# One exponential for the softmax weights of two key tiles in an attention loop

## The chip, the core and the metric

The kernel runs on one core of one Trainium2 chip. The metric is the device time of one execution in microseconds (us), lower is better. The engines are named as in the profile: PE (TensorE, the matrix engine), PEld (its weight loads), DVE (VectorE), ACT (ScalarE), POOL (GpSimd) and SP (SyncE, which here only issues DMAs).

## The reference

Four images of 64 x 64 positions with 256 channels go through two layers. The first is a deformable convolution with a residual. The second takes each image as 4096 tokens and adds an attention and then a gated feed-forward block. The change lies in the attention alone:

```python
def _L1_attn_ref(inputs, Wt, Wx, bh, Wa, ba):
    q = jnp.einsum('bld,du->blu', inputs, Wt)
    k = jnp.einsum('bld,ud->blu', inputs, Wx)
    beta = jnp.tanh(q[:, :, None, :] + k[:, None, :, :] + bh)
    alpha = jnp.einsum('bqku,u->bqk', beta, Wa[:, 0]) + ba[0]
    a = jax.nn.softmax(alpha, axis=-1)
    c_r = jnp.einsum('bqk,bkd->bqd', a, inputs)
    return c_r
...
t = t + _L1_attn_ref(_ln_t(t), L1_attn_Wt, L1_attn_Wx, L1_attn_bh, L1_attn_Wa, L1_attn_ba)
```

For each pair of a query and a key the score is a weighted sum of 32 hyperbolic tangents; the softmax over keys then weights the tokens.

## The kernel before

The images are handled one after the other. For each there is a stage of preparation and then the attention loop, `attention(n, v, [sampling])`. While the loop of image n runs, pieces of the sampling of image n + 1 (the convolution of the first layer) are mixed in as "side" work; the last image has no successor, so its loop runs without side work.

The scores are not made with tanh. The 32 units are split into six groups, taken as three "pairs"; in each group the sum of the tanh terms is a quotient of two sums that PE can make as matrix products. For one key tile (128 keys) and one block of 512 queries, the kernel does for each pair p = 1, 2, 3:

- D: PE makes the denominators d (128 x 1024, two PSUM banks; `below_line`), and N: the numerators nn (two halves of 128 x 512, named a and b; `above_line`). Pairs 1 and 2 take two matmuls for d and one for each half of nn, pair 3 twice that.
- L and E: ACT turns d into 1/d as exp(-ln d): a logarithm (line 1289) writes a new buffer r from d, an exponential (line 1291) works on r in place.
- m: DVE multiplies each half of r with its nn (`quotient`, line 1207).

Then the three r are added: s12 (POOL, line 1295) adds the second to the first, s3a (POOL, line 1297) and s3b (DVE, line 1299) add the third in two halves, and sum (DVE, line 1302) adds the two halves of 512 columns into a buffer et. W (`weigh`) is the exponential of et in place, on ACT (line 1214): these are the softmax weights of the key tile. V (`gather_values`) lets PE multiply weights with values (line 1230): groups of eight key tiles are collected, and for each of four rows of queries the eight tiles are summed in PSUM, two tiles in each V and two V in each step. `hand_over` ("out", once a step) adds a finished sum to acv on DVE (line 1252, or 1250 for the first group of a query block), or, where nothing is finished, takes up one waiting item of the end of a query block: a divide (lines 1261 and 1262, which needs a tile tr loaded by SP), or row statistics.

There are 8 query blocks with 32 key tiles each, so 256 steps ("tiles" b) in the loop of one image and 1024 in the program. The order on each engine is written out as lanes of operations with lags in tiles, and a small planner pops them in turn; nearly every instruction is held in that order. ACT's lane is the first one:

```python
        order = [
            [("L2", 0), ("L1", 0), ("E2", 0), ("E1", 0), ("L3", 0), ("E3", 0), ("W", 2)],
            [("N1a", 1), ("D2", 0), ("N1b", 1), ("Va", 3), ("N2a", 1), ("D1", 0), ("N2b", 1), ("N3a", 1), ("Vb", 3),
             ("D3", 0), ("N3b", 1), ("fill", 0)],
            [("m1a", 1), ("m1b", 1), ("m2a", 1), ("side", 0), ("s3b", 2), ("again", 1), ("m2b", 1), ("sum", 2),
             ("m3a", 1), ("m3b", 1), ("out", 3)],
            [("s12", 1), ("s3a", 1)],
        ]
```

So on ACT the weight exponential of tile b stands between the third exponential of tile b + 2 and the first logarithm of tile b + 3. On DVE the side work of the sampling (copies at lines 828 and 909, products and sums of gathered rows at lines 779 and 783) stands between the product m2a and s3b.

The buffers that matter: d has two (of two banks each), nn two banks, r six (`rp`, three for each tile), et 17 of 2 KB per partition (`ep`, 2 x 8 + 1), tr four of 1 KB. Loads of keys (kf), queries (qf) and tr are issued by SP in its own order.

Of the kernel before, what the change touches and what calls it, by code (L numbers as in the profile page):

```python
# [10 lines left out]
F32 = mybir.dt.float32  # L11
R32 = mybir.dt.float32r
I32 = mybir.dt.int32
AF = mybir.ActivationFunctionType
# [4 lines left out]
P = 128  # L19
NB, H, W, C = 4, 64, 64, 256  # L20
# [21 lines left out]
PVB = 8  # L42
# [9 lines left out]
def layers_kernel(ctx: ExitStack, tc: tile.TileContext, a, out: bass.AP):  # L52
    nc = tc.nc
# [109 lines left out]
    with tc.tile_pool(name="selp", bufs=1) as sp, tc.tile_pool(name="ps_c", bufs=2, space=PSUM) as ps_c:  # L163
# [16 lines left out]
        acc = sp.tile([P, P], F32, name="acc")  # L180
# [59 lines left out]
    def rows(i):  # L240
        return slice(i * P, (i + 1) * P)
# [4 lines left out]
    S = SimpleNamespace(gather=True, hold=False, fills=None, left=0, tables=[], listing=True)  # L246

    @contextmanager
    def scope(*pools):

        with ExitStack() as st:
            for name, bufs, psum in pools:
                kw = {"space": PSUM} if psum else {}
                setattr(S, name, st.enter_context(tc.tile_pool(name=name, bufs=bufs, **kw)))
            yield
            for name, _, _ in pools:
                delattr(S, name)

    keep = tc.keep_in_program_order
# [722 lines left out]
    def row_stats(mv, row, vec=nc.vector):  # L982
        st = S.sb.tile([P, 6], F32, tag="st", name="st2")
        vec.bn_stats(st, row)
        vec.bn_aggr(mv, st)
# [143 lines left out]
    def attention(n, v, beside):  # L1129
# [58 lines left out]
        def below_line(b, pair):  # L1188

            d = S.ps_d.tile([P, 2, 512], F32, tag="d", name="d")  # L1190
            for j in range(2):
                product(d[:, j, :], b, 0, 2 * pair - 2 + j)
            if pair == 3 and b % NT == NT - 1 and b + 1 < nb:
                for which, p in ((0, 3), (1, 1), (1, 2)):
                    queries(b // NT + 1, which, p)
            return d

        def above_line(b, pair, j):

            nn = S.ps_n.tile([P, 512], F32, tag="n", name="nn")  # L1200
            product(nn, b, 1, 2 * pair - 2 + j)
            if pair == 3 and j == 1 and b % NT == NT - 1 and b + 1 < nb:
                queries(b // NT + 1, 1, 3)
            return nn

        def quotient(r, nn, j):
            keep(nc.vector.tensor_tensor(r[:, j, :], nn, r[:, j, :], ALU.mult))  # L1207

        ets, acc, pend, due, rest, late = {}, {}, [], [], [], [0]

        def weigh(b):
            keep(nc.scalar.activation(ets[b], ets[b], AF.Exp))  # L1214
            size = tail.get(b, PVB if b % PVB == PVB - 1 and b < nb - PVB else 0)
            if size:
                pend.extend((b - size + 1, size, j, h) for j in range(4) for h in range(size // 2))
# [18 lines left out]
        def hand_over():  # L1236

            if not due:
                if rest:
                    if len(rest) == late[0]:  # L1240
                        late[0] -= 1
                    rest.pop(0)()
                return
            q, k0, last, j, pv = due.pop(0)
            if j == 0 and k0 == 0:
                ac_t = S.ap.tile([P, 4, C + 1], F32, tag="acv", name="acv")
                acc["sum"] = ac_t
            ac = acc["sum"]
            if k0 == 0:
                keep(nc.vector.tensor_copy(ac[:, j, :], pv))  # L1250
            else:
                keep(nc.vector.tensor_add(ac[:, j, :], ac[:, j, :], pv))  # L1252
            if last:
                i = 4 * q + j
                tr = S.sb.tile([P, C], F32, tag="tr", name="tr", bufs=4)
                nc.sync.dma_start(out=tr, in_=t_d[n][rows(i)])
                t2 = S.sb.tile([P, C], F32, tag="tt", name="t2", bufs=4)

                def divide():
                    es = S.sb.tile([P, 1], F32, tag="es", name="es")  # L1260
                    keep(nc.vector.reciprocal(es, ac[:, j, C:]))
                    keep(nc.vector.scalar_tensor_tensor(t2, ac[:, j, :C], es, tr, ALU.mult, ALU.add))
                    nc.sync.dma_start(out=t2_d[n][rows(i)], in_=t2)

                rest.insert(len(rest) - late[0], divide)
                rest.append(lambda: row_stats(tmv[:, i, :], t2, pinned))
                late[0] += 1
# [9 lines left out]
        rs, ds, ns = {}, {}, {}  # L1277

        def emit(op, b):

            nonlocal second
            p = int(op[1]) if op[1:2].isdigit() else 0
            if op[0] == "D":
                ds[b, p] = below_line(b, p)
            elif op[0] == "N":
                ns[b, op] = above_line(b, p, "ab".index(op[2]))
            elif op[0] == "L":
                rs[b, p] = S.rp.tile([P, 2, 512], F32, tag="r", name="r")
                keep(nc.scalar.activation(rs[b, p], ds.pop((b, p)), AF.Ln))  # L1289
            elif op[0] == "E":  # L1290
                keep(nc.scalar.activation(rs[b, p], rs[b, p], AF.Exp, scale=-1.0))  # L1291
            elif op[0] == "m":
                quotient(rs[b, p], ns.pop((b, "N" + op[1:])), "ab".index(op[2]))
            elif op == "s12":
                keep(nc.gpsimd.tensor_tensor(rs[b, 1], rs[b, 1], rs[b, 2], ALU.add))  # L1295
            elif op == "s3a":
                keep(nc.gpsimd.tensor_tensor(rs[b, 1][:, 0], rs[b, 1][:, 0], rs[b, 3][:, 0], ALU.add))  # L1297
            elif op == "s3b":
                keep(nc.vector.tensor_add(rs[b, 1][:, 1], rs[b, 1][:, 1], rs[b, 3][:, 1]))  # L1299
            elif op == "sum":  # L1300
                et = S.ep.tile([P, 512], F32, tag="et", name="et")
                keep(nc.vector.tensor_add(et, rs[b, 1][:, 0], rs[b, 1][:, 1]))  # L1302
                ets[b] = et
            elif op == "W":
                weigh(b)
            elif op[0] == "V":
                gather_values()
            elif op == "out":
                hand_over()
            elif op == "side":  # L1310
                emit("fill", b)
                for side in beside:
                    next(side, None)
            elif op == "fill":
                while S.fills:
                    S.fills.pop(0)()
            elif op == "again":
                second += max(S.left / max(nb - 6 - b, 1) - 1, 0)
                if second >= 1:
                    second = min(second - 1, 1)  # L1320
                    emit("side", b)
# [38 lines left out]
        for step in range(nb + 4):  # L1360
# [6 lines left out]
            while True:  # L1367
                went = False
                for lane in lanes:
                    while lane and ready(*lane[0]):  # L1370
                        op, b = lane.pop(0)
# [353 lines left out]
    for n in range(NB):  # L1725
        with scope(("att", 1, 0), ("smp", 2, 0), ("dn", 1, 0)):
            v = S.att.tile([P, NT, C + 1], F32, name="v")

            sampling = sample_image(n + 1) if n + 1 < NB else iter(())
            S.gather, S.hold = False, True  # L1730
            with scope(
                ("one", 1, 0), ("two", 2, 0), ("sb", 2, 0), ("row", 2, 0), ("rp", 11, 0),
                ("ps_d", 2, 1), ("ps_n", 1, 1), ("ps_m", 3, 1),
            ):


                main = feed_forward(n - 1, pinned) if n else iter(())
                prep = attention_prep(n, v, pinned)
                listing = (list_tokens(i) for i in range(1, NB))
                if n:  # L1740
                    turns = (
                        "mos" + "m" * 3 + "mo" * 8 + "om" + "oss" * 2 + "m" + "o" * 10 + "m" + "o" * 3
                        + ("m" + "o" * 3 + "m" * 4) * 3
                    )
                else:
                    turns = "oo" + "ool" * 3 + "oo" + "s" + "os" * 24
                for turn in turns:
                    next({"m": main, "o": prep, "s": sampling, "l": listing}[turn], None)
                for rest in (main, prep):
                    for _ in rest:  # L1750
                        pass
            S.gather, S.hold = True, False
            with scope(
                ("two", 2, 0), ("sb", 2, 0), ("ep", 2 * PVB + 1, 0), ("rp", 6, 0), ("ap", 1, 0), ("qp", 16, 0), ("kp", 4, 0),
                ("ps_d", 2, 1), ("ps_n", 2, 1), ("ps_v", 1, 1), ("ps_m", 1, 1),
            ):
                attention(n, v, [sampling])
        attention_any(n)
        if n + 1 < NB:
            sample_any(n + 1)  # L1760
# [39 lines left out]
```

## Time and profile before

| what | value |
|---|---|
| median of 3 runs | 9245.01 us (9230.27 to 9249.85) |
| the profiled execution | 9240.03 us, span 9238.3 us |
| busy share of the span | PE 88%, DVE 77%, ACT 79%, POOL 55% |
| weight exponential, line 1214 | 1024 instructions, mean 614 ns, 628.7 us busy |
| exponential of r, line 1291 | 3072 instructions, mean 1055 ns, 3133.3 us busy |
| logarithm, line 1289 | 3072 instructions, mean 1015 ns, 3066.3 us busy |
| attention loops, first to last weight exponential | 1317 to 2996, 3343 to 5021, 5371 to 7047, 7388 to 8974 us |

The four loops take together some 6.6 of the 9.2 ms. Shares over the whole span are averages over unlike stages, so the loops are read by themselves. A row's duration runs from the start of an instruction to its last write; where two follow each other on ACT, the second starts before the first has ended, so the distance from start to start is what an instruction costs its engine. In the timelines a row "x2" is two instructions of one kind in a stretch, with the time of the whole; what stands in square brackets is idle time ahead of the row and what ended it.

### The profile page before, as it was taken

The page shows a single profiled execution, that of the slowest core. Times are in us where ns is not written, and L with a number is a line of the kernel's source. Part 1 is how long each engine was busy: PE and PEld are TensorE (multiplying, and loading weights), DVE is VectorE, ACT ScalarE, POOL GpSimd, SP SyncE. Part 2 cuts the span into 40 slices and gives each one's busy share as a digit, 9 for nine tenths or more (in the row PEclk, how much of TensorE's full clock was granted, in tenths as well). Part 3 has the DMA queues.
Part 4 walks back from the last instruction along what each step waited for, and adds up shares of the span by engine and source line. Part 5 has one row for each costly group of instructions (what it writes and reads, how often), then busy time and mean ns, then how long its engine had stood idle before and what let it go on. Part 6 is the DMA issues. An engine that isn't in the chain of part 4 may idle for free. (4 is left out here: it accounts for less than half of the span.)

```text
span 9238.3 us, 139629 instructions
## 1 busy us (share of the span) xinstructions
PE 8127.6 (88%) x46154; PEld 5830.1 (63%) x46154; DVE 7094.9 (77%) x13053; ACT 7294.4 (79%) x8590; POOL 5075.3 (55%) x3108
## 2 busy tenths in 40 slices
PE   5777779999999599999997799999996899999995
PEld 3555547777776267777775367777774466666663
DVE  4545559998988569999987479999987388888872
ACT  2344269999999379999997489999996499999982
POOL 0122247777766157777764267777663266666652
PEclk8888779999999799999999799999998899999997
DMA  3455565555542545555533555555533533333322
GB/s 113 133 165 166 156 203 153 152 149 151 153 131 87 201 148 153 152 149 157 157 117 98 188 151 154 159 153 154 145 110 105 193 102 105 103 103 103 112 71 83
DMA packets 1575709, 1279.14 MB, mean 138 GB/s; under 512 B 123522, under 2 KB 1407140, under 8 KB 1574948
## 3 DMA queue, kind: packets, MB, share of 16 engines
q1 hardware_dynamic: 1411940, 958.70, 35.0%
q10 hardware_dynamic: 123264, 190.67, 5.7%
q0 software_dynamic: 39744, 120.42, 5.6%
q8 instruction: 379, 6.21, 0.3%
q14 instruction: 382, 3.13, 0.1%
HBM read 1011.33 MB, written 285.79 MB: 140 GB/s over the span
## 5 line engine op out<-in xcount | busy, mean ns | idle before, releaser
L1207 DVE TENSOR_TENSOR r<-nn,r 128x512 f32<-128x512 f32 x6144 | 4107.5, 686 | 716.9 <-PE nn L1184 522.8
L1295 POOL TENSOR_TENSOR r<-r 128x1024 f32<-128x1024 f32 x1024 | 2719.7, 2656 | 1727.5 <-DVE r L1207 1350.6
L1184 PE MATMUL nn<-qf,kf 128*128 128x512 f32 x8192 | 3221.9, 441 | 201.0 <-DVE r L1207 67.5
L1289 ACT ACTIVATE r<-d 128x1024 f32<-128x1024 f32 x3072 | 3066.3, 1015 | 277.9 <-DVE r L1299 177.1
L1291 ACT ACTIVATE r<-r 128x1024 f32<-128x1024 f32 x3072 | 3133.3, 1055 | 32.5
L1184 PE MATMUL d<-qf,kf 128*128 128x512 f32 x8192 | 2546.7, 412 | 48.7 <-ACT r L1289 31.9
L1184 PEld LDWEIGHTS nn<-qf,kf 128*128 128x128 f32 x8192 | 1454.3, 188 | 1197.2 <-DVE r L1207 889.1
L1230 PE MATMUL pv<-v,et 128*128 128x257 f32 x8192 | 2143.2, 384 | 35.5 <-DVE acv L1252 35.5
L1230 PEld LDWEIGHTS pv<-v,et 128*128 128x128 f32 x8192 | 1527.9, 190 | 353.1 <-DVE acv L1252 52.7
L1184 PEld LDWEIGHTS d<-qf,kf 128*128 128x128 f32 x8192 | 1491.4, 189 | 392.3 <-ACT r L1289 117.5
L1297 POOL TENSOR_TENSOR r<-r 128x512 f32<-128x512 f32 x1024 | 1333.1, 1302 | 83.9 <-DVE r L1207 3.9
L1299 DVE TENSOR_TENSOR r<-r 128x512 f32<-128x512 f32 x1024 | 715.6, 699 | 14.0 <-POOL r L1295 13.8
L1302 DVE TENSOR_TENSOR et<-r 128x512 f32<-128x512 f32 x1024 | 703.4, 687 | 10.3 <-POOL r L1297 10.3
L767 POOL DMA_INDIRECT ga<-xt,tii x576 | 588.2, 1021 | 207.3 <-issue 84.3
L1214 ACT ACTIVATE et<-et 128x512 f32<-128x512 f32 x1024 | 628.7, 614 | 22.3 <-DVE et L1302 22.3
L871 PE MATMUL ptq<-ident,wq 128*120 128x128 f32 x2048 | 313.4, 281 | 80.9 <-ACT ac L830 48.0
L871 PEld LDWEIGHTS ptq<-ident,wq 128*120 128x120 f32 x2048 | 291.0, 183 | 133.7 <-ACT ac L830 49.8
L913 POOL TENSOR_TENSOR xr<-ac,xr 128x256 f32<-128x256 f32 x32 | 27.5, 859 | 558.6 <-ACT ac L912 558.5
L270 PE MATMUL pc<-xn,diag 32*32 32x256 f32 x9216 | 260.7, 424 | 63.5 <-issue 39.8
L1611 POOL DMA_INDIRECT sort<-v,rif x128 | 129.2, 1009 | 339.9 <-DVE rif L270 211.7
L864 POOL TENSOR_TENSOR xr<-xr,outb 128x256 f32<-128x256 f32 x128 | 99.9, 781 | 329.8 <-DMA xr<-in_x_dram 284.7
L270 DVE TENSOR_TENSOR raw<-po,omb 128x432 f32<-128x432 f32 x64 | 34.3, 598 | 302.7 <-PE po L270 302.7
(355 smaller groups left out, 5974.4 us busy)
## 6 DMA issues: line engine op xcount, KB each, us to landing
kf<-k SPq DMA_DIRECT2D x4096, 128.0 KB
wq<-band SPq DMA_DIRECT2D x256, 480.0 KB
v<-t SPq DMA_DIRECT2D x64, 512.0 KB
k<-kh ACTq DMA_DIRECT2D x128, 256.0 KB
qf<-n SPq DMA_DIRECT2D x256, 128.0 KB
xw<-xt SPq DMA_DIRECT2D x256, 120.0 KB
qf<-q SPq DMA_DIRECT2D x224, 128.0 KB
wc<-w ACTq DMA_DIRECT2D x32, 848.0 KB
```

The lines of the kernel that those rows point to most:

```text
L767: keep(nc.gpsimd.indirect_dma_start(out=ga[:, s].rearrange("p c e -> p (c e)"), out_offset=None, in_=line, in_offset=bass.IndirectOffsetOn ...
L871: keep(nc.tensor.transpose(pt[:HALF, g, :], wq[:, 4 * f + g, :], ident))
L1184: keep(nc.tensor.matmul(dst, ks[b][:, blk, :].bitcast(R32), moving, start=(i == 0), stop=(i == len(blocks) - 1)))
L1207: keep(nc.vector.tensor_tensor(r[:, j, :], nn, r[:, j, :], ALU.mult))
L1214: keep(nc.scalar.activation(ets[b], ets[b], AF.Exp))
L1230: keep(nc.tensor.matmul(pv, ets[b0 + i][:, rows(j)], v[:, k0 + i, :], start=(i == 0), stop=(i == size - 1)))
L1289: keep(nc.scalar.activation(rs[b, p], ds.pop((b, p)), AF.Ln))
L1291: keep(nc.scalar.activation(rs[b, p], rs[b, p], AF.Exp, scale=-1.0))
L1295: keep(nc.gpsimd.tensor_tensor(rs[b, 1], rs[b, 1], rs[b, 2], ALU.add))
L1297: keep(nc.gpsimd.tensor_tensor(rs[b, 1][:, 0], rs[b, 1][:, 0], rs[b, 3][:, 0], ALU.add))
L1299: keep(nc.vector.tensor_add(rs[b, 1][:, 1], rs[b, 1][:, 1], rs[b, 3][:, 1]))
L1302: keep(nc.vector.tensor_add(et, rs[b, 1][:, 0], rs[b, 1][:, 1]))
```

## The change

Two key tiles, an even one and the odd one after it, share one buffer of 128 x 2 x 512. DVE's sum writes the half that belongs to its tile. The weight exponential is left out behind even tiles; behind odd ones a single instruction of 1024 columns handles both halves. Its place in ACT's order is that of the odd tile's exponential. The pool `ep` has 9 buffers of 4 KB in place of 17 of 2 KB, and tr three buffers in place of four.

```diff
-        ets, acc, pend, due, rest, late = {}, {}, [], [], [], [0]
+        ets, pairs, acc, pend, due, rest, late = {}, [], {}, [], [], [], [0]
 
         def weigh(b):
-            keep(nc.scalar.activation(ets[b], ets[b], AF.Exp))
+            if b % 2:
+                pair = pairs.pop()
+                keep(nc.scalar.activation(pair, pair, AF.Exp))
             size = tail.get(b, PVB if b % PVB == PVB - 1 and b < nb - PVB else 0)
...
-                tr = S.sb.tile([P, C], F32, tag="tr", name="tr", bufs=4)
+                tr = S.sb.tile([P, C], F32, tag="tr", name="tr", bufs=3)
...
             elif op == "sum":
-                et = S.ep.tile([P, 512], F32, tag="et", name="et")
-                keep(nc.vector.tensor_add(et, rs[b, 1][:, 0], rs[b, 1][:, 1]))
-                ets[b] = et
+                if b % 2 == 0:
+                    pairs.append(S.ep.tile([P, 2, 512], F32, tag="et", name="et"))
+                ets[b] = pairs[-1][:, b % 2]
+                keep(nc.vector.tensor_add(ets[b], rs[b, 1][:, 0], rs[b, 1][:, 1]))
...
-                ("two", 2, 0), ("sb", 2, 0), ("ep", 2 * PVB + 1, 0), ("rp", 6, 0), ("ap", 1, 0), ("qp", 16, 0), ("kp", 4, 0),
+                ("two", 2, 0), ("sb", 2, 0), ("ep", PVB + 1, 0), ("rp", 6, 0), ("ap", 1, 0), ("qp", 16, 0), ("kp", 4, 0),
```

## The prediction

> **What bounds the kernel now.** I first read the busy time by slice on the page, then the windows, to find the stages. The four attention loops are the stretches of nines, and the last differs from the first three.
>
> ```profile
> PE   5777779999999599999997799999996899999995
> ACT  2344269999999379999997489999996499999982
> ```
>
> ```profile
> 1617.00:1848.00 231.00, 225.00 (x1084) 167.21 (x1082) 212.98 (x372) 219.64 (x245) 166.58 (x103) 1.00 0.55 153
> 7854.00:8085.00 231.00, 224.19 (x889) 157.98 (x888) 198.10 (x337) 229.83 (x260) 148.53 (x75) 1.00 0.35 103
> ```
>
> The columns are PE, weight loads, DVE, ACT, POOL, granted clock, DMA share, GB/s. In the last loop ACT is busy 229.83 of 231 us: it alone sets the pace. In the first three, where the sampling of the next image runs beside, ACT has 11 us free in 231. The list of waits says for what, in the first loop (1330 to 2990 us) and then in the last (7400 to 8970 us):
>
> ```profile
> ACT r L1289 <- DVE r L1299: 58.5, 104, 2.3
> ```
>
> ```profile
> ACT et L1214 <- DVE et L1302: 1.4, 1, 1.4
> ```
>
> So 104 of 256 tiles of the first loop make a logarithm (Ln) wait for DVE's s3b (line 1299), which frees the buffer that it writes; the last loop has no such wait. The ACT timeline of the last loop prices each instruction by the distance from start to start:
>
> ```profile
> 8000.42 1.92 ACT L1289 ACTIVATE r<-d 128x1024 f32<-128x1024 f32 x2
> 8002.23 2.00 ACT L1291 ACTIVATE r<-r 128x1024 f32<-128x1024 f32 x2
> 8004.13 1.02 ACT L1289 ACTIVATE r<-d 128x1024 f32<-128x1024 f32 x1
> 8005.18 1.06 ACT L1291 ACTIVATE r<-r 128x1024 f32<-128x1024 f32 x1
> 8006.15 0.61 ACT L1214 ACTIVATE et<-et 128x512 f32<-128x512 f32 x1
> 8006.67 1.92 ACT L1289 ACTIVATE r<-d 128x1024 f32<-128x1024 f32 x2
> ```
>
> Two Ln take 1.81 us, two exponentials of 1024 columns 1.90 (0.95 each), the third Ln 1.05, the third exponential 0.97, the weight exponential of 512 columns 0.52 (its row says 0.61, but the next instruction starts before it ends). The sum, 6.25 us, is the tile's period there.
>
> Now the same engine in the first loop, and DVE beside it:
>
> ```profile
> 1505.86 0.61 ACT L1214 ACTIVATE et<-et 128x512 f32<-128x512 f32 x1
> 1506.37 1.00 ACT L1289 ACTIVATE r<-d 128x1024 f32<-128x1024 f32 x1
> 1507.54 1.03 ACT L1289 ACTIVATE r<-d 128x1024 f32<-128x1024 f32 x1 [0.16 <-DVE r L1299]
> 1508.46 2.00 ACT L1291 ACTIVATE r<-r 128x1024 f32<-128x1024 f32 x2
> ...
> 1512.36 0.61 ACT L1214 ACTIVATE et<-et 128x512 f32<-128x512 f32 x1
> 1512.88 2.07 ACT L1289 ACTIVATE r<-d 128x1024 f32<-128x1024 f32 x2
> ```
>
> ```profile
> 1506.74 0.68 DVE L1299 TENSOR_TENSOR r<-r 128x512 f32<-128x512 f32 x1
> ...
> 1510.49 2.12 DVE L1207 TENSOR_TENSOR r<-nn,r 128x512 f32<-128x512 f32 x3 [0.67 <-ACT r L1291]
> 1512.53 0.28 DVE L828 COPY ac<-pmq 128x128 f32<-128x128 f32 x1
> 1512.73 0.48 DVE L783 TENSOR_REDUCE so<-ga 128x32 f32<-128x192 f32 x1
> 1513.13 0.68 DVE L1299 TENSOR_TENSOR r<-r 128x512 f32<-128x512 f32 x1
> ...
> 1516.29 0.41 DVE L1252 TENSOR_TENSOR acv<-acv,pv 128x257 f32<-128x257 f32 x1
> ```
>
> This is a ring: s3b ends at 1507.42, the second Ln starts 0.12 later, its two exponentials end at 1510.46, DVE starts three products at 1510.49, does sampling work (0.28 and 0.48), then the next s3b, ending at 1513.81; the next second Ln starts at 1513.92 (its row of two ends at 1514.95, less 1.03). That is 6.38 us around, and the weight exponential isn't in it: it lies in the time that ACT has over. Without sampling work the ring is about 0.6 shorter and ACT's 6.25 decides.
>
> **The change.** Each loop loses 256 exponentials of 512 columns and gains 128 of 1024, behind odd tiles. In the program as built PE, DVE and POOL keep their order; on ACT the even tiles' exponentials are gone and the double one stands in the odd ones' places; on SP some loads of tr shift.
>
> *ACT's work:* per pair 2 x 0.52 = 1.04 becomes 0.95 (same shape and operands as L1291): 0.09 less, 512 x 0.09 = 46 us in all. But it is divided unevenly: the step after an even tile needs 6.25 - 0.52 = 5.73, the step after an odd one 5.73 + 0.95 = 6.68.
>
> *Even steps, first three loops:* nothing is won where the second Ln waits for s3b; it waits 0.52 longer. Parity can be read: two gathers a step make acv ready every second step, so the step with L1252 (or L1250) ahead of its products follows an even tile. Going through the ACT and DVE timelines tile by tile, in about 85 of 100 even steps the second Ln is at or within 0.05 us of s3b's release. Counting for each only what it stood behind that release, up to 0.52, gives 0.04 a step: 384 x 0.04 = 15 us gained, between 0 and 15.
>
> *Odd steps, first three loops:* the first Ln comes 0.43 later. From second Ln to second Ln an odd step took 6.55 on the mean of 121 readable steps of the first loop (6.55 and 6.54 in the other two), an even one 6.67. ACT now needs 6.68; lifting only the shorter odd steps to that adds 0.25 a step (half of them were at ACT's own 6.25 and take the whole 0.43, those with a wait above 0.43 take nothing): 384 x 0.25 = 96 us. A part is absorbed where DVE isn't ready for the exponentials anyway, since divides (L1261, L1262) or row statistics (L270) precede the products: taking off the time from the exponential's end to DVE's start leaves 0.16, 61 us. But that DVE work hangs on PE's four d matmuls, which in the median odd step start 0.10 after the first Ln ends, so it is pushed as well. I take 0.20: 77 us, between 61 and 96.
>
> *Last loop:* s3b ends 0.66 to 0.79 before the second Ln, of which 0.12 is the signal: some 0.55 of cover for the 0.52 by which an even step comes early. ACT then keeps its stream and wins 128 x 0.09 = 11.5; where the cover fails by the few hundredths that are left, nothing. I take 9, between 0 and 11.5.
>
> *Ends of the loops:* the last double exponential stands before the last weighted sums: 4 x 0.43 = 2 us.
>
> *Weights later by a step, buffers:* the even tile's weights come a tile later, but the value matmuls take groups of eight, whose last pair had to wait for the odd tile already; the waits show no pv behind ACT. A pair's buffer returns after 18 tiles where a single one returned after 17, and DVE's sum (L1302) waits for POOL alone. Nothing. The double exponential waits for the odd sum, as the single one did; behind it on ACT stands the next tile's first Ln (8 such waits in the whole trace, 22.3 us, at the loops' ends). With three tr buffers the fourth load of a query block waits for the first divide, six steps ahead of its own; in SP's order it still stands about three tiles ahead of its use, with key loads queued behind it that are as early. No divide of before waits for a load. So nothing; without that cover one divide in each of 32 query blocks would come up to a step late, 32 x 6.6 = 211 us if all of it reached the ring.
>
> A rule of the Trainium skill speaks on both sides here. Perfetto Trace Analysis, "Optimizing Scalar/DVE Operations", says that larger operations help a saturated engine, with 93 ns of overhead for an instruction of ScalarE on SBUF. By that the sum would be 512 x 0.093 = 48 us faster, an estimate from the page that agrees with the 0.09 of the rows. The same section says that an engine that isn't saturated but makes others wait may do better with instructions broken up; ACT's 219.64 of 231 is that case for three loops, and by this the change goes the wrong way there.
>
> Sum: -15 + 77 - 9 + 2 = +55 us. The profiled execution took 9240.03 (span 9238.3): 9295. The median of the runs lies 5 above it: 9300.
>
> **Rivals.**
> A, ACT is the bound everywhere: its 95% share in three loops speaks for it, the 104 waits against. All 46 us are won: about 9199.
> B, the lead of the even step carries over: if the PE and DVE work that it brings forward shortens the next ring by the 0.25, only the last loop's gain is left: 0 to -12, some 9239. For it, DVE also waits for PE's nn (52.3 us in 145 waits between 1500 and 2500 us); against it, nn has two banks, freed by the very products.
> C, the whole 0.43 is lost in every pair of three loops, because even steps are already at the ring and odd ones fall behind with d as well: 384 x 0.43 = 165, and the last loop wins nothing: 9410. It decides if odd steps that waited over 0.43 also grow. Against it, half of the odd steps had a wait to spend.
> The built order excludes that the exponentials are not halved.
>
> **How the numbers follow.** Forecast 0.62, A 0.13, B 0.15, C 0.10. The forecast's own range is 61 - 15 - 12 = +34 to 96 + 2 = +98: 9279 to 9343 around the runs' median. The range of 8 in 10 takes in B and the lower part of C and leaves out A: 9235 to 9360. About 0.2%, 18.5 us, is what a measurement can tell from no change: faster is A (0.13), same is B (0.15), slower the rest (0.72).
>
> **What would show it.** In the profile after: the weight exponential (line 1216 there) with 512 instructions of about 1.06; in the first three loops ACT's idle time before the Ln (line 1291 there) for s3b above the 177 us that it is in all now, nearly all of it behind even tiles, and odd steps of 6.68 or more; pairs of about 13.4 us where they took 13.2; the last loop at about 12.4 a pair, ACT still full. Wrong, if the first three loops shorten, if the last one lengthens, or if the divides wait for tr.

## The result, and the profile after

The changed kernel takes 9298.55 us (median of 6 runs, 9280.39 to 9308.5) where before takes 9245.52 (6 runs, 9230.27 to 9249.85): slower by a factor of 1.006, 95% interval 1.0049 to 1.0072. The profiled execution of after took 9301.64 us.

Line numbers below the change are two to four higher: the Ln stands at line 1291, the exponential of r at 1293, s3b at 1301, sum at 1306, and the weight exponential at 1216. Its group on the page of after, with that of the Ln:

```profile
L1291 ACT ACTIVATE r<-d 128x1024 f32<-128x1024 f32 x3072 | 3062.7, 1015 | 399.7 <-DVE r L1301 302.4
L1216 ACT ACTIVATE et<-et 128x1024 f32<-128x1024 f32 x512 | 533.5, 1042 | 25.2 <-DVE et L1306 25.2
```

Busy time of the weight exponential fell from 628.7 to 533.5 us, but ACT's idle time ahead of the Ln rose from 277.9 to 399.7, of which the wait for s3b rose from 177.1 to 302.4. In the windows (first loop, last loop) ACT is less busy than it was in the first loop, 213.63 us against 219.64, and as full as before in the last:

```profile
1617.00:1848.00 231.00, 223.20 (x1081) 164.84 (x1082) 209.06 (x368) 213.63 (x224) 163.33 (x100) 1.00 0.56 151
7854.00:8085.00 231.00, 224.18 (x893) 160.89 (x891) 197.22 (x337) 229.83 (x242) 149.73 (x76) 1.00 0.36 107
```

The waits of the first loop (1330 to 2990 us) on ACT:

```profile
ACT r L1291 <- DVE r L1301: 99.4, 122, 2.8
```

It was 58.5 us in 104 waits. Of the 302.4 us in all, 273.5 stand in front of the second Ln behind even tiles and 28.9 behind odd ones; before it was 120.3 and 56.8. ACT's timeline in the first loop shows the uneven steps:

```profile
1858.39 1.04 ACT L1216 ACTIVATE et<-et 128x1024 f32<-128x1024 f32 x1
1859.34 1.01 ACT L1291 ACTIVATE r<-d 128x1024 f32<-128x1024 f32 x1
1860.81 1.03 ACT L1291 ACTIVATE r<-d 128x1024 f32<-128x1024 f32 x1 [0.47 <-DVE r L1301]
1861.74 1.99 ACT L1293 ACTIVATE r<-r 128x1024 f32<-128x1024 f32 x2
1863.63 1.01 ACT L1291 ACTIVATE r<-d 128x1024 f32<-128x1024 f32 x1
1864.67 1.06 ACT L1293 ACTIVATE r<-r 128x1024 f32<-128x1024 f32 x1
1865.64 1.00 ACT L1291 ACTIVATE r<-d 128x1024 f32<-128x1024 f32 x1
1867.67 1.03 ACT L1291 ACTIVATE r<-d 128x1024 f32<-128x1024 f32 x1 [1.03 <-DVE r L1301]
1868.60 2.00 ACT L1293 ACTIVATE r<-r 128x1024 f32<-128x1024 f32 x2
1870.49 1.01 ACT L1291 ACTIVATE r<-d 128x1024 f32<-128x1024 f32 x1
1871.54 1.06 ACT L1293 ACTIVATE r<-r 128x1024 f32<-128x1024 f32 x1
1872.50 1.04 ACT L1216 ACTIVATE et<-et 128x1024 f32<-128x1024 f32 x1
1873.45 1.92 ACT L1291 ACTIVATE r<-d 128x1024 f32<-128x1024 f32 x2
```

Behind an even tile no weight exponential stands (1864.67, then at once the next Ln at 1865.64), and the time that this leaves is spent waiting: the second Ln at 1867.67 has idled 1.03 us for s3b. Behind the odd tile at 1872.50 nothing is waited for: the two Ln follow each other, and the second one starts at 1874.35 (its row of two ends at 1875.37, less 1.02), 6.68 us after the second Ln of the step before. That is the sum of ACT's own work.

The table gives each attention loop in the profiled execution, in us from the start of the first to the start of the last of DVE's products (line 1207), and the median of the runs. The experiments follow below it. The runs of before beside them had medians of 9239.46 (for e1, e2, e5 and e6) and 9237.6 us (for e3, e4 and e7).

| kernel | loop 1 | loop 2 | loop 3 | loop 4 | median us | ratio to before, 95% |
|---|---|---|---|---|---|---|
| before | 1686.8 | 1687.2 | 1684.5 | 1595.2 | 9245.52 | |
| after | 1710.6 | 1711.4 | 1716.7 | 1587.9 | 9298.55 | 1.0049 to 1.0072 |
| e1_buffers | 1685.3 | 1689.8 | 1685.5 | 1595.2 | 9247.31 | 0.9999 to 1.0017 |
| e2_two_together | 1717.6 | 1719.2 | 1716.9 | 1594.9 | 9336.18 | 1.0095 to 1.0125 |
| e3_even_place | 1697.6 | 1698.5 | 1693.8 | 1589.0 | 9272.09 | 1.0021 to 1.0044 |
| e4_last_loop | 1685.5 | 1686.4 | 1687.9 | 1588.5 | 9240.18 | 0.9991 to 1.0008 |
| e5_seven_single | 1675.1 | 1673.2 | 1671.4 | 1594.6 | 9210.32 | 0.9960 to 0.9981 |
| e6_seven_pair | 1676.4 | 1677.1 | 1673.4 | 1587.8 | 9197.13 | 0.9943 to 0.9967 |
| e7_seven_last | 1672.8 | 1670.8 | 1670.6 | 1588.3 | 9194.32 | 0.9940 to 0.9967 |

After loses 24, 24 and 32 us in the first three loops and wins 7 in the last.

### The profile page after: what moved, and what is told of

Read it like the earlier page. It is cut to its first block, busy times and chain, and to the rows that moved or that the text cites. A ratio compares the mean times of both kernels' runs of the same rounds, so it can differ in the third digit from the quotient of the medians.

```text
span 9299.6 us, 139122 instructions
## 1 busy us (share of the span) xinstructions
PE 8142.4 (88%) x46154; PEld 5841.3 (63%) x46154; DVE 7082.4 (76%) x13053; ACT 7243.9 (78%) x8078; POOL 5075.7 (55%) x3108
## 5 line engine op out<-in xcount | busy, mean ns | idle before, releaser
L1291 ACT ACTIVATE r<-d 128x1024 f32<-128x1024 f32 x3072 | 3062.7, 1015 | 399.7 <-DVE r L1301 302.4
L1184 PEld LDWEIGHTS d<-qf,kf 128*128 128x128 f32 x8192 | 1516.2, 189 | 454.3 <-ACT r L1291 167.8
L1299 POOL TENSOR_TENSOR r<-r 128x512 f32<-128x512 f32 x1024 | 1332.5, 1301 | 84.0 <-DVE r L1207 3.9
L1216 ACT ACTIVATE et<-et 128x1024 f32<-128x1024 f32 x512 | 533.5, 1042 | 25.2 <-DVE et L1306 25.2
```

The lines of the kernel that those rows point to most:

```text
L1184: keep(nc.tensor.matmul(dst, ks[b][:, blk, :].bitcast(R32), moving, start=(i == 0), stop=(i == len(blocks) - 1)))
L1216: keep(nc.scalar.activation(pair, pair, AF.Exp))
```

## Experiments

All edits are against the changed kernel.

**The buffers alone (e1_buffers).**

```diff
-            if b % 2:
-                pair = pairs.pop()
-                keep(nc.scalar.activation(pair, pair, AF.Exp))
+            keep(nc.scalar.activation(ets[b], ets[b], AF.Exp))
```

> Shared buffers and three tr buffers as in the change, but each tile's 512-column exponential by itself in its old place. Theory (uneven ACT steps cost the time): the time of before, 9245 +- 10, and ACT waits before Ln for s3b of some 177 us in total. Rival (the buffers, or the later tr loads, cost it): 9290 to 9300.

Measured: 9247.31 us, ratio 1.0008 with an interval that holds 1, and the wait for s3b is that of before (the group of the Ln on its page):

```profile
L1289 ACT ACTIVATE r<-d 128x1024 f32<-128x1024 f32 x3072 | 3066.2, 1015 | 280.5 <-DVE r L1299 177.7
```

Its loops are those of before within 3 us. So neither the shared buffers nor the missing fourth tr buffer costs anything that shows (the interval leaves room for at most 16 us); the loss comes with the double exponential.

**Two narrow ones in the wide one's place (e2_two_together).**

```diff
             if b % 2:
-                pair = pairs.pop()
-                keep(nc.scalar.activation(pair, pair, AF.Exp))
+                for k in (b - 1, b):
+                    keep(nc.scalar.activation(ets[k], ets[k], AF.Exp))
```

> Shared buffers, and behind odd tiles the two 512-column exponentials one after the other, so ACT does as much as before, but in uneven steps: 5.73 us after an even tile, 6.25 + 0.52 = 6.77 after an odd one. Theory (unevenness costs): slower than the change, by up to 0.09 in each of 384 pairs of the first three loops (+35) and 0.09 in each of the last loop's 128 (+11): 9325 to 9345. Rival (the wide instruction, or its single wait for two sums, costs): 9245 or up to 9260.

Measured: 9336.18 us, 1.011 times before and within the expected 9325 to 9345. ACT runs the very instructions of before; one in each pair only comes a tile later. That alone costs 31 to 33 us in each of the first three loops of the table and nothing in the last (1594.9 against 1595.2). The loss therefore comes from the uneven steps and not from a wide instruction; the wide one wins a part of it back.

**The double one a tile later (e3_even_place).**

```diff
-            if b % 2:
-                pair = pairs.pop()
+            if b and b % 2 == (b >= nb - 7):
+                pair = pairs.pop(0)
```

> The change, with the double exponential one tile later: in the place of the next even tile's exponential (the last eight tiles of a loop keep the odd place), so that even steps need 6.68 us of ACT and odd ones 5.73. Theory (the loss is what the long step lacks in waiting time): in the trace of before, even steps wait more, so lifting them costs 0.19 and not 0.25 a step, and of the odd steps' 0.52 some 0.10 is won and not 0.04; 128 x (0.19 - 0.10) = 12 us a loop, times 3, less 7 in the last loop: about 9270, 20 to 30 us faster than the change. Rival (the double instruction costs what it costs wherever it stands): 9290 to 9305, as the change.

Measured: 9272.09 us, where 9270 was expected and the change takes 9298.55. Against the runs of before beside each, this kernel loses 34 us and the change 53, so it is some 19 us faster, just short of the expected 20 to 30. The first three loops lose 9 to 11 us each in place of 24 to 32. From second Ln to second Ln in the middle of the first loop, a step behind an even tile rose from 6.74 to 6.92 on the mean and one behind an odd tile fell from 6.57 to 6.48, some +0.17 and -0.09, where 0.19 and 0.10 had been read off the trace of before. The long step hurts less where the wait for s3b was longer: before, it was 120.3 us behind even tiles and 56.8 behind odd ones.

**A seventh buffer for r, with single exponentials (e5_seven_single) and double ones (e6_seven_pair).** One pair buffer of the weights is given up for it. Both kernels have this edit, and the first that of e1_buffers too:

```diff
-            "L": (6, lambda op, b: [{"1": ("sum", b), "2": ("s12", b), "3": ("s3b", b)}[op[1]]]),
+            "L": (7, lambda op, b: [{"1": ("sum", b), "2": ("s12", b), "3": ("s3b", b)}[op[1]]]),
...
-                ("two", 2, 0), ("sb", 2, 0), ("ep", PVB + 1, 0), ("rp", 6, 0), ("ap", 1, 0), ("qp", 16, 0), ("kp", 4, 0),
+                ("two", 2, 0), ("sb", 2, 0), ("ep", PVB, 0), ("rp", 7, 0), ("ap", 1, 0), ("qp", 16, 0), ("kp", 4, 0),
```

> One exponential per tile as before, but seven buffers for r in place of six (8 pair buffers for the weights in place of 9 make room). Theory (a ring s3b -> second Ln -> exponentials -> products -> s3b sets the first three loops): a seventh buffer frees the second Ln from s3b, so those waits go (177 us to under 40) and the three loops get shorter towards ACT's 6.25 us a tile; 0.36 above that now, so at most 768 x 0.36 = 276 us, and I take half: 9110, between 8970 and 9200; last loop unchanged. Rival (PE and DVE are the bound and the wait is a symptom): 9235 to 9255.

> The change with seven buffers for r (and 8 pair buffers). Theory (the ring keeps the even step's lead from being used): with the ring loosened the loss against one exponential per tile goes, and with ACT as the bound up to 512 x 0.09 = 46 us are won against the seven-buffer run with single exponentials: 10 to 46 us faster than that run. Rival (uneven steps cost by themselves, whatever the buffers): 40 to 70 us slower than that run, as the change is against before.

ACT's longest waits in the first loop (1330 to 2990 us), first with single, then with double exponentials:

```profile
ACT r L1289 <- PE d L1184: 31.9, 99, 1.6
ACT r L1289 <- POOL r L1295: 8.0, 10, 1.6
```

```profile
ACT r L1291 <- PE d L1184: 54.2, 81, 2.3
ACT r L1291 <- PE nn L1184: 9.3, 9, 2.2
```

The wait for s3b has left both lists. With single exponentials the three loops became 12 to 14 us shorter each (in the fastest of this kernel's eight runs, 9190.59) and the median 9210.32: the right way, but far short of the expected 9110, and outside both the theory's range and the rival's. So the ring is one limit of these loops and not the only one. ACT now waits for PE's d, for half of the time that had gone to s3b. PE and DVE in turn go on waiting for each other over nn, in the same stretch of the first loop, here first before and then with seven buffers and single exponentials:

```profile
PEld nn L1184 <- DVE r L1207: 192.9, 411, 3.1
DVE r L1207 <- PE nn L1184: 109.4, 269, 1.5
```

```profile
PEld nn L1184 <- DVE r L1207: 186.0, 361, 3.3
DVE r L1207 <- PE nn L1184: 129.8, 324, 1.7
```

Whether this exchange through the two nn buffers holds d back, and so is the second limit, no run separates.

For the pairs the main part of the expectation came out: the three loops of e6_seven_pair are 1 to 4 us longer than those of e5_seven_single (3 to 6 longer than those of e7_seven_last below, which has single exponentials there), where with six buffers pairs cost 24 to 32. What uneven steps cost depends on the number of r buffers. With six the second Ln stands at s3b and a short step's lead is lost: from second Ln to second Ln a step behind an even tile fell by only 0.07 and one behind an odd tile rose by 0.26 in the middle of the first loop, after against before. With seven a good part of the lead is used: -0.19 and +0.20 there, e6_seven_pair against e5_seven_single. The other part, up to 46 us won because ACT would be the bound, didn't come: the pairs win nothing in the first three loops, and only the last loop's 7 us are left. The medians, 9197 and 9210, differ by 13; the loops of the two traces add up to 7 us of loss and 7 of gain, so how much the pairs win over the whole program with seven buffers stays open.

**Pairs in the last loop alone, with six buffers (e4_last_loop) and with seven (e7_seven_last).**

```diff
-            if b % 2:
+            if n + 1 < NB:
+                keep(nc.scalar.activation(ets[b], ets[b], AF.Exp))
+            elif b % 2:
```

> Double exponentials in the last loop only, single ones in the first three. Theory (the last loop alone is bound by ACT): its gain in the change's trace stays and the losses go: 7 us faster than the run with shared buffers and single exponentials, 9235 to 9243. Rival (the last loop's 7 us came from how the earlier loops ended): 9245 to 9250.

> Seven buffers for r, double exponentials in the last loop only. Theory (with seven buffers the ring no longer sets the first three loops, and ACT doesn't either): single and double are the same there, so this is within 8 us of the run with seven buffers and pairs everywhere, 9190 to 9205, and some 7 faster than seven buffers with single exponentials. Rival (uneven steps still cost in the first three loops): 15 or more faster than the run with pairs everywhere.

With six buffers the time, 9240.18, can't be told from before. In the trace the last loop is 6.7 us shorter and the first three are unchanged within 4, so the last loop's gain is its own; in the total it stays below what these runs resolve. With seven buffers the median is 9194.32, three below the run with pairs everywhere: the same, as expected, and 16 below e5_seven_single, where some 7 were expected and the last loop of the trace gives 6. Both seven-buffer kernels with pairs beat before by about 0.45% (intervals 0.33 to 0.60) and after by some 100 us.

## Why the prediction came out

**Sum and sign.** Forecast were +55 and 9300; measured were 53 us between the medians and 9298.55. How near it came is in part luck. In the profiled executions the first three loops lost 80 us together where 62 were forecast, and the last won 7; but what lies outside the four loops was 12 us shorter than before, which no term of the sum had, so these executions differ by 62 us. This rest varies from 2573 to 2595 us among the nine kernels of the table. The main line held: the change loses in the three loops with side work and wins in the last, and e1_buffers shows that buffers and tr loads cost nothing, as was put down for them. In the trace of after, DVE's divides wait 1.7 us in all for a tr load, and 1.8 in that of e1_buffers.

**Odd and even steps.** For the comparison, the second Ln of a row of two is taken to start 1.02 us before the row's end, as in the prediction's example, in the middle of the first loop, about 100 steps of each kind. Before: 6.74 behind even and 6.57 behind odd tiles. After: 6.67 and 6.83. So an odd step grew by 0.26, just above the 0.16 to 0.25 that the prediction allowed, and an even step shrank by 0.07 where 0.04 was put down. The two deviations offset each other in part: 128 x (0.26 - 0.07) = 24 us a loop, where 128 x (0.20 - 0.04) = 20 was forecast. The median odd step is now 6.68, as worked out from the rows of before, and 79 of 102 odd steps have no wait left in front of their second Ln. The part that the late divides and row statistics were to absorb was hardly absorbed. PE's d waits longer for ACT's Ln, 43.6 us against 22.1 between 1400 and 2900 us (weight loads of d), which fits the caution that d is pushed as well; how much of the lost time goes by d and how much by the second Ln itself no run separates.

**Last loop.** The term of 9, at most 11.5, was somewhat large: the trace gives 7.3. The price itself was right: on the mean of the middle of this loop a single exponential takes 0.519 us from its start to the next one's (before), a double one 0.948 (after), and 2 x 0.519 - 0.948 = 0.09. But the pair's period fell only from 12.485 to 12.43, by some 0.055. The cover was thinner than the prediction read: in 27 of 110 even steps of before s3b ends less than 0.64 us ahead of the second Ln, and 0.64 is the signal's 0.12 and the 0.52. In after the second Ln of 31 of 110 short steps stands over 0.05 us late, all but one of them 0.12 behind the end of s3b. The row of the two Ln shows it, here 2.00 behind an even tile and 1.92 behind an odd one:

```profile
8105.50 2.00 ACT L1291 ACTIVATE r<-d 128x1024 f32<-128x1024 f32 x2
8112.25 1.92 ACT L1291 ACTIVATE r<-d 128x1024 f32<-128x1024 f32 x2
```

```profile
8105.68 0.68 DVE L1301 TENSOR_TENSOR r<-r 128x512 f32<-128x512 f32 x1
```

No idle time is listed for it, since the first Ln's row hasn't ended yet. With seven buffers 14 of 110 stand over 0.05 late, none by more than 0.07, and the pair's period there is 12.42.

**Rivals.** A (46 us won everywhere) fell: in the first three loops the wait for s3b took up more than ACT's saved time. B (the lead carries over) is in good part what happens with seven buffers and doesn't with six. C (0.43 lost in every pair, 165 us) is about twice the 80 lost, since odd steps had waits to spend, as e3_even_place shows from the other side.

**The skill's rule.** The Trainium skill, Perfetto Trace Analysis, "Optimizing Scalar/DVE Operations", recommends larger operations for a saturated engine and says that breaking instructions up may help where the engine isn't saturated but holds others up. The first half agrees with the trace: the last loop, with ACT at 229.83 of 231 us, became 7 us shorter. The second half isn't shown here: the other three loops became 24 to 32 us longer with the larger operation, but e2_two_together, which breaks it up in the same place, is slower still (31 to 33). The moment counts, and the width only by what it saves.

## What to carry to other kernels

Before merging two small instructions of alternate steps, don't only count the time saved: lay out the engine's short and its long step singly, and ask whether a wait for a buffer eats the short one's lead and whether the long one finds a wait to hide in. Where neither helps, one more buffer in the ring may be worth more than the merge. If the merge stays, choose its place: behind the step that had waited longest it cost less than half in the loops where it lost.

## What was not expected

Taking away ACT's largest wait in the first three loops (58.5 us in the first) shortened each by only 12 to 14 us, since ACT then waited for PE's d. And where ACT was full, a pair won 0.055 us of the 0.09 that the double exponential saves: the short step's second Ln came up against s3b there too, by delays of less than 0.1 us in nearly every case, which the lists of waits don't show.
